# Block products for half of batch 6 as well, a denser two-batch product, and a written order for the last halves

## The chip, the cores and the metric

The kernel runs on one core of a Trainium2 chip. The metric is the device time of the whole program in microseconds. A run has one profiled execution, taken by the hardware profiler; its span goes from the first instruction to the last.

## The reference

```python
# _layernorm, gelu, rsqrt: the usual ones
def layer0(x, ada_emb):                    # x (8, 1024, 512), ada_emb (8, 512)
    ae = _layernorm(ada_emb, ln_g, ln_b)
    h = gelu(ae @ w1 + b1)
    x_a, x_b = split(h @ w2 + b2, 2)       # each (8, 512, 8)
    layer = base_layer + einsum('bdr,bkr->bdk', x_a, x_b)
    return x + einsum('btc,bco->bto', x, layer)

def layer1(x, y):
    ys = y / sqrt(512)
    d = rsqrt(einsum('bi,io->bo', ys * ys, weight * weight) + 1e-8)
    return einsum('bsi,io->bso', x * ys[:, None, :], weight) * d[:, None, :]

x = x + layer0(x, cond_1024)
out = x + layer1(x, cond_1024)
```

Everything after the small conditioning part is linear in x, so the kernel forms one 512 x 512 matrix per batch, q[b], and multiplies x[b] (1024 x 512) by it.

## The kernel before

Float32 products are made of three matmuls: each operand is split into a rounded part (ScalarE, a cast to float32r) and the rest (VectorE, a subtraction), and high x high, high x rest and rest x high are added in PSUM.

*Start.* The first 80 us load the weights, compute the conditioning and make q[0] to q[3]. This stretch is not touched by the change.

*Main tiles.* `main(b, t)` (L811) computes 128 rows of output: 4 chunks of the inner dimension x 3 = 12 matmuls of 512 columns into a `po` bank, a ScalarE copy, and a store of 256 KB issued by ScalarE. There are 8 tiles per batch; the text counts them through, tile 8b + t, from 0 to 55 for batches 0 to 6. `load_x` (L663) brings half a batch of x (1 MB) through SP's queue into the pool `big`, which has nine buffers; `split_x` (L667) splits the columns of two tiles. The matrices q[b] and the split x (`xs`) live in `big` as well. `split_p` (L651) splits q[b] into `ph` and `pl`.

*Making the next matrices.* Between main tiles, lists of work (`at`, L945) make q[4] to q[7]. `Pair` (L547) makes two batches' matrices, 4 with 5 and 6 with 7, by seven block products instead of eight, in the order `(1, 2, 5, 6, 3, 7, 4)`. A product has two units of six matmuls of 512 columns. `early` makes a right operand on VectorE, `prepare` rounds and splits it. Two units share banks of the pool `acc` (four banks): product 5 takes the banks of product 2 once VectorE has added those into q. One unit stands behind each main tile. `rank_term` (L514) adds the rank-8 part: four small matmuls (`pr`) into four `acc` banks and four additions on VectorE. `load_rank` (L505) fetches its operands by eight transfers that POOL issues, and `load_d` two rows for `Pair`.

*The last batch.* `Seven` (L823) computes batch 7 by seven block products with the Winograd form of Strassen's scheme, on blocks of half the inner dimension and half the columns. `make_right` makes four sums of blocks of q[7] and splits all right operands. `make_left(g)` does the same for x. `part(g)` runs the products in the order 1, 5, 6, 2, 7, 3, 4, each 12 matmuls of 256 columns, and writes 512 rows of output as two tiles `o1` and `o2` of 512 KB. Products 1, 6, 7 and 4 add onto one bank (`sw`), 5 and 3 onto another (`sz`), 2 has its own (`sv`). Between them the bank is read: a copy on ScalarE (L915, L917, L919, L928) or an addition on VectorE (L921, L923, L925). The block that follows on the same bank waits for that read. In the last part product 4 is copied and stored in two pieces (L912).

*Order.* TensorE's matmuls stand in text order. In the first 80 us VectorE and ScalarE do too (`InOrder.on`); from L805 on a scheduler orders them, with its own estimate of times. A wrapper `ve`, `se`, `sy` pins an instruction only while `InOrder.on` is set; `nc.vector` and `nc.scalar` are never pinned. Pools that the end needs (`late`) open when the pools of the making are closed (`late_pools`, L937).

Of the kernel before, what the change touches and what calls it, by code (L numbers as in the profile page):

```python
# [7 lines left out]
F32 = mybir.dt.float32  # L8
F32R = mybir.dt.float32r
# [5 lines left out]
P = 128  # L15
NB = 8
NT = 1024
D = 512
# [12 lines left out]
def cond_resid_kernel(ctx: ExitStack, tc: tile.TileContext, small, cond, condrows, consts,  # L31
# [791 lines left out]
    class Seven:  # L823
# [5 lines left out]

        ORDER = (1, 5, 6, 2, 7, 3, 4)

        def __init__(self, b):
            self.b, self.left = b, {}

        def make_right(self):
            b, late = self.b, pools["late"]
            t = late.tile([P, 4, 2, HD], F32R, tag="tl", name=f"tl_{b}", bufs=1)  # L840
            h = late.tile([P, 4, 2, HD], F32R, tag="th", name=f"th_{b}", bufs=1)
            raws = late.tile([P, 4, 2, HD], F32, tag="sums", name=f"traw_{b}", bufs=2)
            t1, t2, t3, t4 = (raws[:, i] for i in range(4))
            b11, b12 = q[b][:, 0:2, 0:HD], q[b][:, 0:2, HD:D]
            b21, b22 = q[b][:, 2:4, 0:HD], q[b][:, 2:4, HD:D]
            p_tiles(b)
            for rows, cols in ((slice(0, 4), slice(0, HD)), (slice(2, 4), slice(HD, D))):
                nc.scalar.copy(ph[b][:, rows, cols], q[b][:, rows, cols])
                nc.vector.tensor_sub(pl[b][:, rows, cols], q[b][:, rows, cols],
                                     ph[b][:, rows, cols].bitcast(F32))  # L850
            for o, x, y in ((t1, b12, b11), (t2, b22, t1), (t3, b22, b12), (t4, b21, t2)):
                nc.vector.tensor_sub(o, x, y)
            for i in range(0, 4, 2):
                at = slice(i, i + 2)
                nc.scalar.copy(h[:, at], raws[:, at])
                nc.vector.tensor_sub(t[:, at], raws[:, at], h[:, at].bitcast(F32))
            self.right = {5: (h[:, 0], t[:, 0]), 6: (h[:, 1], t[:, 1]), 7: (h[:, 2], t[:, 2]),
                          4: (h[:, 3], t[:, 3])}
            for p, rows, cols in ((1, slice(0, 2), slice(0, HD)), (2, slice(2, 4), slice(0, HD)),
                                  (3, slice(2, 4), slice(HD, D))):  # L860
                self.right[p] = ph[b][:, rows, cols], pl[b][:, rows, cols]

        def make_left(self, g):
            b, late = self.b, pools["late"]
            at = slice(2 * P * g, 2 * P * (g + 1))
            top, low = raw[b, 0][:, :, at], raw[b, 1][:, :, at]
            a11, a12, a21, a22 = top[:, 0:2], top[:, 2:4], low[:, 0:2], low[:, 2:4]
            s = late.tile([P, 4, 2, 2 * P], F32R, tag="sl", name=f"sl_{b}_{g}", bufs=2)
            h = late.tile([P, 4, 2, 2 * P], F32R, tag="sh", name=f"sh_{b}_{g}", bufs=2)
            x = late.tile([P, 2, 2, 2 * P], F32R, tag="x22", name=f"x22_{b}_{g}", bufs=2)  # L870
            xa = big.tile([P, 2, KC, 2 * P], F32R, tag="big", name=f"xa_{b}_{g}")
            nc.scalar.copy(xa[:, 0], top)
            nc.vector.tensor_sub(xa[:, 1], top, xa[:, 0].bitcast(F32))
            raws = late.tile([P, 4, 2, 2 * P], F32, tag="sums", name=f"sraw_{b}_{g}", bufs=2)
            s1, s2, s3, s4 = (raws[:, i] for i in range(4))
            nc.vector.tensor_add(s1, a21, a22)
            nc.vector.tensor_sub(s2, s1, a11)
            for i, (o, u, v) in enumerate(((s3, a11, a21), (s4, a12, s2))):
                nc.vector.tensor_sub(o, u, v)
            for i in range(0, 4, 2):  # L880
                two = slice(i, i + 2)
                nc.scalar.copy(h[:, two], raws[:, two])
                nc.vector.tensor_sub(s[:, two], raws[:, two], h[:, two].bitcast(F32))
            nc.scalar.copy(x[:, 0], a22)
            nc.vector.tensor_sub(x[:, 1], a22, x[:, 0].bitcast(F32))
            self.left[g] = {5: (h[:, 0], s[:, 0]), 6: (h[:, 1], s[:, 1]), 7: (h[:, 2], s[:, 2]),
                            3: (h[:, 3], s[:, 3]), 4: (x[:, 0], x[:, 1]),
                            1: (xa[:, 0, 0:2], xa[:, 1, 0:2]), 2: (xa[:, 0, 2:4], xa[:, 1, 2:4])}

        def product(self, g, p, bank, m, first):  # L890
            (lh, ll), (rh, rl) = self.left[g][p], self.right[p]
            for kk in range(2):
                for i, (a, r) in enumerate(((lh, rh), (lh, rl), (ll, rh))):
                    mm(bank[:, m, :], a[:, kk, m * P:(m + 1) * P], r[:, kk, :],
                       start=(first and m == 0 and kk == 0 and i == 0),
                       stop=(kk == 1 and i == 2), skip_group_check=True)

        def part(self, g, last):
            b, bank = self.b, {}
            o1, o2 = (pools["late"].tile([P, 2, D], F32, tag="o2", name=f"o{i}_{b}_{g}", bufs=3)  # L900
                      for i in range(2))
            for p in self.ORDER:
                key = {5: "z", 3: "z", 2: "v"}.get(p, "w")
                first = p in (1, 5, 2)
                if first:
                    pool, tag = (acc, "acc") if key == "v" else (po, "po")
                    bank[key] = pool.tile([P, 2, HD], F32, tag=tag, name=f"s{key}_{b}_{g}")
                u = bank[key]
                for m in range(2):
                    self.product(g, p, u, m, first)  # L910
                    if p == 4 and last:
                        nc.scalar.copy(o2[:, m, 0:HD], u[:, m])  # L912
                        self.store(o2, g, 1, slice(m, m + 1))
                if p == 1:
                    nc.scalar.copy(o1[:, :, 0:HD], u)  # L915
                elif p == 5:
                    nc.scalar.copy(o2[:, :, HD:D], u)  # L917
                elif p == 6:
                    nc.scalar.copy(o1[:, :, HD:D], u)  # L919
                elif p == 2:  # L920
                    nc.vector.tensor_add(o1[:, :, 0:HD], u, o1[:, :, 0:HD])  # L921
                elif p == 7:
                    nc.vector.tensor_add(o2[:, :, HD:D], u, o2[:, :, HD:D])  # L923
                elif p == 3:
                    nc.vector.tensor_add(o1[:, :, HD:D], u, o1[:, :, HD:D])  # L925
                    self.store(o1, g, 0, slice(0, 2))
                elif not last:
                    nc.scalar.copy(o2[:, :, 0:HD], u)  # L928
                    self.store(o2, g, 1, slice(0, 2))

        def store(self, o, g, half, ms):
            at = half * HT + 2 * P * g
            nc.scalar.dma_start(
                out[self.b, at + P * ms.start:at + P * ms.stop, :].rearrange("(m p) d -> p m d", p=P),
                o[:, ms, :])

# [15 lines left out]
    place = lambda i: divmod(i, NTT)  # L952
    for b in range(1, 4):
        first = (b - 1) * NTT
        at(*place(max(0, 4 * b - 8)), load_rank, b)
        at(*place(4 * b - 2), rank_term, b)
        for j in range(2):
            at(*place(first + 3 + j), split_p, b, j)
    for b, first in ((4, 13), (6, 30)):

        at(*place(first - 9), load_d, b)
        at(*place(first - 6), new_pair, b)
        for n, p in enumerate(Pair.ORDER):
            at(*place(first - 5 + 2 * n), lambda b=b, p=p: pairs[b].early(p))
            at(*place(first - 2 + 2 * n), lambda b=b, p=p: pairs[b].prepare(p))
            for i in range(2):
                at(*place(first + 2 * n + i), lambda b=b: pairs[b].unit())
        at(*place(first + 2), load_rank, b)
        at(*place(first + 4), load_rank, b + 1)
        at(*place(first + 14), rank_term, b)  # L970
        at(*place(first + 15), rank_term, b + 1)
        at(*place(first + 15), split_p, b, 0)
        at(*place(first + 16), split_p, b, 1)
        if b == 4:
            at(*place(first + 19), split_p, b + 1, 0)
            at(*place(first + 21), split_p, b + 1, 1)
    seven = Seven(NB - 1)
    at(*place(46), late_pools)
    at(*place(47), seven.make_right)
    at(*place(49), load_x, NB - 1, 0)  # L980
    at(*place(50), load_x, NB - 1, 1)
    at(*place(52), seven.make_left, 0)
    at(*place(54), seven.make_left, 1)

    for b in range(NB - 1):
        for t in range(NTT):
            if t == 0 and b + 2 < NB:
                p_tiles(b + 1)
            main(b, t)
            i = b * NTT + t  # L990
            if t % 4 == 0 and i + 4 < (NB - 1) * NTT:
                load_x(*divmod(i // 4 + 1, NHALF))
            if t % 2 == 0 and i + 4 < (NB - 1) * NTT:
                split_x(*divmod(i // 2 + 2, NTT // 2))
            for f, args in after.get((b, t), ()):
                f(*args)
    for g in range(2):
        seven.part(g, g == 1)


# [67 lines left out]
```

## Time and profile before

| | |
|---|---|
| median of 3 runs | 302.77 us (302.65 to 303.15) |
| profiled execution | 302.81 us |
| its span | 301.0 us |
| TensorE matmul, busy | 294.3 us, 1429 matmuls |
| VectorE, busy | 194.0 us, 287 instructions |
| ScalarE, busy | 150.2 us, 218 instructions |
| GpSimd, busy | 34.8 us |
| data moved | 62.12 MB, mean 206 GB/s |
| main tiles end, block products start | 276.35 us |

How to read it: PE is TensorE, PEld its weight loads, DVE VectorE, ACT ScalarE, POOL GpSimd; ACTq is the queue on which ScalarE issues transfers. The helper lines L45 and L62 record every matmul and most of the elementwise work, so groups are told apart by tiles: `po` main tiles, `pp` the two-batch products, `pr` rank terms, `sw`, `sz`, `sv` the block products of the end. `o` is an output tile in SBUF. A row of the timeline is start, duration, engine, line, operation and tiles, and in brackets the idle time before it with what ended it. Matmuls are pipelined, so that one takes longer (0.28 us) than the step to the next (0.12 us). The span's last TensorE matmul starts at 297.10.

### The profile page before, as it was taken

What the parts mean: (1) busy time and instruction counts of PE and PEld (TensorE: products, weight loads), DVE (VectorE), ACT (ScalarE), POOL (GpSimd) and SP (SyncE); (2) the same over time, 40 slices, a digit from 0 to 9 for tenths busy, and PEclk for the clock granted to TensorE, in tenths of its full rate; (3) what the DMA queues carried; (4) which work ended last, traced back from release to release, by engine and by line L of the source; (5) the groups of instructions that cost most, each with busy time, mean ns of one, the idle gap of its engine ahead of it and who ended that gap; (6) DMA issues with size and microseconds to landing.
All of it is one profiled execution on the core that took longest, in us unless ns stands there. A gap on an engine that the chain in (4) does not pass through costs nothing.

```text
span 301.0 us, 3809 instructions
## 1 busy us (share of the span) xinstructions
PE 294.3 (98%) x1429; PEld 224.8 (75%) x1429; DVE 194.0 (64%) x287; ACT 150.2 (50%) x218; POOL 34.8 (12%) x74
## 2 busy tenths in 40 slices
PE   7999999999999999999999999999999999999994
PEld 2655465466878778888888877888888877888993
DVE  4779750979569889794157549994356238994201
ACT  4756132256566672572457535664465436855130
POOL 0011000057104505100000018000000000000000
PEclk9999999999999999999999999999999999999999
DMA  6999999696519888186124347725144364432033
GB/s 207 412 426 418 407 423 416 216 327 182 197 70 312 320 250 273 72 244 210 69 89 193 87 192 188 233 82 199 50 194 152 128 209 140 165 117 93 12 143 139
DMA packets 19027, 62.12 MB, mean 206 GB/s; under 512 B 2736, under 2 KB 2992, under 8 KB 14656
## 3 DMA queue, kind: packets, MB, share of 16 engines
q1 hardware_dynamic: 6064, 38.78, 34.6%
q10 hardware_dynamic: 9168, 16.78, 15.0%
q0 software_dynamic: 3776, 6.31, 7.7%
q8 instruction: 11, 0.18, 0.2%
q14 instruction: 8, 0.07, 0.1%
HBM read 44.02 MB, written 17.84 MB: 206 GB/s over the span
## 4 chain that ended last, share of the span: by engine, by line
PE 86%; DMA 5%; DVE 5%; ACT 2%; issue 1%; SPq 0%; ACTq 0%
PE po L45 51%; PE pp L45 13%; PE pq L45 7%; PE sw L45 4%; DMA w<-in_w 4%; PE px L45 3%; PE pg L45 2%; PE sz L45 2%; DVE n L62 2%; DMA b_raw<-in_baseT 2%; PE pr L45 1%; PE sv L45 1%; PE pt_t L45 1%; ACT work L62 1%; DVE scr L62 0%
## 5 line engine op out<-in xcount | busy, mean ns | idle before, releaser
L45 PE MATMUL po<-ph,xs 128*128 128x512 f32 x448 | 144.9, 391 | 0.0
L45 PEld LDWEIGHTS po<-ph,xs 128*128 128x128 f32 x448 | 84.1, 188 | 19.3 <-issue 1.7
L45 PE MATMUL po<-pl,xs 128*128 128x512 f32 x224 | 87.3, 390 | 0.0
L62 ACT COPY o<-po 128x512 f32<-128x512 f32 x56 | 32.8, 586 | 60.8 <-PE po L45 60.8
L45 PEld LDWEIGHTS po<-pl,xs 128*128 128x128 f32 x224 | 42.1, 188 | 8.6
L62 DVE TENSOR_TENSOR xs<-x,xs 128x1024 fp32r<-128x1024 f32 x28 | 34.0, 1220 | 10.5 <-ACT xs L62 10.5
L62 DVE TENSOR_TENSOR nl_p<-n,nh_p 128x1024 fp32r<-128x1024 f32 x14 | 17.1, 1222 | 23.1 <-ACT nh_p L62 23.0
L62 ACT CAST xs<-x 128x1024 fp32r<-128x1024 f32 x28 | 29.1, 1052 | 1.2 <-DMA x<-in_x 1.0
L62 DVE TENSOR_TENSOR q<-pr,q 128x512 f32<-128x512 f32 x32 | 20.1, 684 | 13.6 <-PE pr L45 13.6
L511 POOL DMA_DIRECT2D fa<-kept_a x28 | 13.7, 506 | 77.9 <-PE pr L45 77.2
L45 PE MATMUL pq<-nh,bh 128*128 128x512 f32 x48 | 19.8, 412 | 0.0
L45 PE MATMUL pq<-nl,bh 128*128 128x512 f32 x48 | 19.1, 398 | 0.1
L62 ACT COPY q<-pp 128x512 f32<-128x512 f32 x20 | 11.7, 587 | 14.9 <-PE pp L45 14.1
L45 PE MATMUL pq<-nh,bl 128*128 128x512 f32 x48 | 18.9, 394 | 0.0
L62 DVE SCALAR_TENSOR_TENSOR n<-w_sb,ysT,d 128x512 f32<-128x512 f32 x24 | 17.7, 746 | 1.5 <-DMA d<-d_out 1.5
L62 DVE TENSOR_TENSOR pl<-q,ph 128x1024 fp32r<-128x1024 f32 x14 | 16.9, 1220 | 0.1
L62 ACT CAST nh_p<-n 128x1024 fp32r<-128x1024 f32 x14 | 14.7, 1052 | 3.5 <-DVE n L62 1.9
L62 ACT CAST ph<-q 128x1024 fp32r<-128x1024 f32 x14 | 14.6, 1053 | 3.4 <-DVE q L62 3.1
L45 PE MATMUL px<-w,hT 128*32 128x512 f32 x128 | 16.0, 601 | 0.1
L45 PEld LDWEIGHTS pq<-nh,bh 128*128 128x128 f32 x48 | 9.0, 188 | 8.4 <-issue 5.0
L511 POOL DMA_DIRECT2D ft<-kept_t x28 | 13.8, 512 | 4.9 <-DMA kept_t<-st_t 4.9
L62 ACT CAST nh<-n 128x512 fp32r<-128x512 f32 (+1 forms) x10 | 6.9, 707 | 11.5 <-DVE n L62 11.5
(193 smaller groups left out, 407.1 us busy)
## 6 DMA issues: line engine op xcount, KB each, us to landing
w<-in_w SPq DMA_DIRECT2D x16, 1024.0 KB, 10.7
x<-in_x SPq DMA_DIRECT2D x16, 1024.0 KB, 5.3
out<-o ACTq DMA_DIRECT2D x58, 256.0 KB, 2.1
ft<-kept_t POOLq DMA_DIRECT2D x28, 64.0 KB, 3.4
fa<-kept_a POOLq DMA_DIRECT2D x28, 64.0 KB, 3.2
d<-d_out POOLq DMA_DIRECT2D x6, 256.0 KB, 3.9
out<-o ACTq DMA_DIRECT2D x3, 512.0 KB, 2.9
w_sb<-in_weight SPq DMA_DIRECT2D x2, 512.0 KB, 5.3
```

What stands on the lines that cost most here:

```text
L45: tc.keep_in_program_order(nc.tensor.matmul(*args, **kw))
L62: return lambda *a, **kw: pin(f(*a, **kw)) if InOrder.on else f(*a, **kw)
L511: nc.gpsimd.dma_start(fold[name, b][32 * c:32 * c + 32, :], kept[name, g][32 * i:32 * i + 32, :])
```

## The change

The block products take over the second half of batch 6 (512 rows, main tiles 52 to 55) as well. `Seven` is made for batches 6 and 7, and a part now covers the rows of one half of x, `raw[b, g]`, where it had taken two columns of rows from both halves. `make_right` is divided into `make_sums` and the rest, which batch 6 doesn't need. `make_left` becomes a generator whose steps are put between the products of the part before it. There are three parts: batch 6 half 1, batch 7 half 0, batch 7 half 1. In these parts `InOrder.on` is set, and all elementwise work goes through `ve` and `se`. In the last part the bank `sw` becomes two banks, one for each 128 rows. The scratch pools change their number of buffers.

The product of batches 6 and 7 starts at tile 28 where it started at 30, and has three units per two tiles where it had two. That of 4 and 5 starts at tile 11 where it started at 13. The rank terms of batches 2 to 7, the splits of q[2] to q[6] and the opening of `late` move with them.

```diff
-        def make_right(self):
+        def make_sums(self):
...
-            t = late.tile([P, 4, 2, HD], F32R, tag="tl", name=f"tl_{b}", bufs=1)
-            h = late.tile([P, 4, 2, HD], F32R, tag="th", name=f"th_{b}", bufs=1)
-            raws = late.tile([P, 4, 2, HD], F32, tag="sums", name=f"traw_{b}", bufs=2)
+            t = late.tile([P, 4, 2, HD], F32R, tag="tl", name=f"tl_{b}", bufs=2)
+            h = late.tile([P, 4, 2, HD], F32R, tag="th", name=f"th_{b}", bufs=2)
+            raws = late.tile([P, 4, 2, HD], F32, tag="sums", name=f"traw_{b}", bufs=1)
...
         def make_left(self, g):
...
-            at = slice(2 * P * g, 2 * P * (g + 1))
-            top, low = raw[b, 0][:, :, at], raw[b, 1][:, :, at]
+            top, low = (raw[b, g][:, :, 2 * P * i:2 * P * (i + 1)] for i in range(2))
...
+            def rest(two):
+                ve.tensor_sub(s[:, two], raws[:, two], h[:, two].bitcast(F32))
+
+            se.copy(xa[:, 0], top)
+            se.copy(x[:, 0], a22)
+            ve.tensor_add(s1, a21, a22)
+            ve.tensor_sub(s2, s1, a11)
+            yield
+            se.copy(h[:, 0:2], raws[:, 0:2])
+            ve.tensor_sub(s3, a11, a21)
+            ve.tensor_sub(s4, a12, s2)
+            yield
+            se.copy(h[:, 2:4], raws[:, 2:4])
+            ve.tensor_sub(xa[:, 1], top, xa[:, 0].bitcast(F32))
+            yield
+            rest(slice(0, 2))
+            yield
+            ve.tensor_sub(x[:, 1], a22, x[:, 0].bitcast(F32))
+            yield
+            rest(slice(2, 4))
+            yield
...
+        def part(self, g, steps=(), last=False):
...
             for p in self.ORDER:
...
-                    pool, tag = (acc, "acc") if key == "v" else (po, "po")
-                    bank[key] = pool.tile([P, 2, HD], F32, tag=tag, name=f"s{key}_{b}_{g}")
...
+                    pool, tag = (po, "po") if key == "z" else (acc, "acc")
+                    bank[key] = [pool.tile([P, 2, HD], F32, tag=tag, name=f"s{key}{i}_{b}_{g}")
+                                 for i in range(2 if key == "w" and last else 1)]
+                self.product(g, p, bank[key], first)
...
+                for m, u in enumerate(bank[key]):
+                    u, to = (u, slice(0, 2)) if len(bank[key]) == 1 else (u[:, 0:1], slice(m, m + 1))
+                    if p in (2, 3, 7):
+                        ve.tensor_add(o[:, to, cols], u, o[:, to, cols])
+                    else:
+                        se.copy(o[:, to, cols], u)
+                    if p in (3, 4):
+                        self.store(o, g, int(p == 4), to)
+                next(steps, None)
...
-        at(*place(max(0, 4 * b - 8)), load_rank, b)
-        at(*place(4 * b - 2), rank_term, b)
+        at(*place(max(0, 3 * b - 7)), load_rank, b)
+        at(*place(3 * b - 1), rank_term, b)
...
-    for b, first in ((4, 13), (6, 30)):
+    for b, spots in ((4, [11 + n for n in range(14)]), (6, [28 + 2 * n // 3 for n in range(14)])):
...
+            spot = spots[2 * n]
+            at(*place(spot - 5), lambda b=b, p=p: pairs[b].early(p))
+            at(*place(spot - 2), lambda b=b, p=p: pairs[b].prepare(p))
+        for spot in spots:
+            at(*place(spot), lambda b=b: pairs[b].unit())
...
+        at(*place(end), rank_term, b)
+        at(*place(end + 1), rank_term, b + 1)
+    for b, spot in ((4, 26), (5, 33), (6, 41)):
+        for j in range(2):
+            at(*place(spot + j), split_p, b, j)
...
+    at(*place(40), late_pools)
+    at(*place(42), sevens[0].make_sums)
+    at(*place(43), sevens[0].make_right, True)
+    at(*place(44), load_x, NB - 2, 1)
+    at(*place(45), sevens[1].make_sums)
+    at(*place(47), all_left, 0, 1)
+    at(*place(48), sevens[1].make_right, False)
+    at(*place(48), load_x, NB - 1, 0)
...
+    load_x(NB - 1, 1)
+    InOrder.on = True
+    sevens[0].part(1, sevens[1].make_left(0))
+    sevens[1].part(0, sevens[1].make_left(1))
+    sevens[1].part(1, last=True)
```

## The prediction

> **What bounds the kernel now.** I read the page first (busy shares, slices, chain), then TensorE's matmul starts in order of time, then the busy time by stage around the last two batches, then the last 6 us on every engine and the DMA engines. The profiled execution took 302.81 us; its span is 301.0, so 1.8 us lie around the span. The median of the runs shown is 302.77, so sums made against the profile need a shift of only -0.04.
>
> ```profile
> PE 294.3 (98%) x1429; PEld 224.8 (75%) x1429; DVE 194.0 (64%) x287; ACT 150.2 (50%) x218; POOL 34.8 (12%) x74
> ...
> PE   7999999999999999999999999999999999999994
> ...
> PE 86%; DMA 5%; DVE 5%; ACT 2%; issue 1%; SPq 0%; ACTq 0%
> ```
>
> A busy TensorE is not yet a full one, so I looked at the matmul starts. From 80 us to 295.7 us they follow each other at a constant pitch per shape; the only longer steps are some 0.2 us around each group of four rank matmuls (pr). So in that stretch the time is the number and the shape of the matmuls, and VectorE and ScalarE cost something only where they make TensorE wait. Nothing in the first 88 us changes order.
>
> ```profile
> 180.00:230.00 50.00, 50.00 (x222) 40.80 (x221) 36.52 (x45) 28.22 (x37) 6.96 (x15) 1.00 0.46 151
> ...
> 265.47:276.35 10.88, 10.88 (x50) 9.01 (x48) 9.07 (x11) 5.72 (x8) 0.00 (x0) 1.00 0.27 99
> 276.35:286.43 10.08, 10.08 (x86) 10.08 (x85) 2.08 (x3) 2.35 (x4) 0.00 (x0) 1.00 0.07 28
> ```
>
> These are stretches of the span, with busy time of PE, PEld, DVE, ACT and POOL, then clock, DMA share and GB/s. The second is the last four tiles of batch 6, the third the first half of batch 7 by seven block products: the same amount of output, 10.88 us against 10.08. The clock is 1.00 in both. VectorE has much room in the third row.
>
> The last 6 us are another matter:
>
> ```profile
> 295.66 0.28 PE L45 MATMUL sw<-th,x 128*128 128x256 f32 x1
> 296.40 0.39 PE L45 MATMUL sw<-th,x 128*128 128x256 f32 x1 [0.46 <-ACT o L912]
> 297.10 0.28 PE L45 MATMUL sw<-th,x 128*128 128x256 f32 x1
> ```
>
> ```profile
> 295.98 0.37 ACT L912 COPY o<-sw 128x256 f32<-128x256 f32 x1 [4.45 <-DVE o L925]
> 295.99 0.90 ACTq L933 DMA_DIRECT2D out<-o  x2
> 297.42 0.37 ACT L912 COPY o<-sw 128x256 f32<-128x256 f32 x1 [1.07 <-PE sw L45]
> 297.82 0.35 ACTq L933 DMA_DIRECT2D out<-o  x1
> ```
>
> ```profile
> 296.00:297.00 1.00, 0.60 (x5) 0.60 (x6) 0.00 (x0) 0.35 (x1) 0.00 (x0) 1.00 0.11 41
> 297.00:298.00 1.00, 0.38 (x4) 0.18 (x2) 0.00 (x0) 0.37 (x1) 0.00 (x0) 1.00 1.03 389
> 298.00:299.00 1.00, 0.00 (x0) 0.00 (x0) 0.00 (x0) 0.00 (x0) 0.00 (x0) 1.00 1.01 375
> 299.00:300.00 1.00, 0.00 (x0) 0.00 (x0) 0.00 (x0) 0.00 (x0) 0.00 (x0) 1.00 0.65 244
> ```
>
> TensorE stands still between 295.78 and 296.40, because ScalarE reads the first half of the bank that the next matmuls write. The chain of waits runs through this stall. But the DMA rows say that the stall does not set the end: the stores of 512, 256 and 256 KB are 1 MB, and all 16 DMA engines are full from 296.9 to 299.65. That burst starts 0.9 us after the 512 KB store was issued at 295.99, and that store waits for VectorE's last addition (295.26 to 295.95). The last 256 KB, issued at 297.82, would begin to move at about 298.7 by the same 0.9 us. At 0.67 us for each 256 KB the two stores before it hold the engines from 296.9 to 298.9.
>
> **The change part by part.**
>
> *Four tiles of batch 6 become seven block products.* Removed: 4 x 12 = 48 matmuls of 512 columns, 10.88 us by the second row above, 227 ns each. Added: 7 x 12 = 84 of 256 columns, 10.08 us by the third row, 120 ns each. All of it lies on TensorE, which sets the time: -0.80 us. Rule against row: the trace has the pitch at 227 and 120 ns. The Trainium skill ("TensorE: Matmul & The Clock Gate", Back-to-back issue gap) gives an isolated pitch of columns / 2.4 GHz plus 2.5 ns, so 215.8 and 109.2 ns. By that the change would be worth 48 x 0.2158 - 84 x 0.1092 = 10.36 - 9.17 = 1.19 us. Each matmul here costs about 11 ns more than the rule, and the change adds 36 of them net; the row decides, 0.80.
>
> *Evictions and stores of those tiles.* Four ScalarE copies of 0.59 and four 256 KB stores go. Four copies, three VectorE additions of 0.69 and two 512 KB stores come, as in batch 7 today. They lie beside the products: 0.
>
> *Sums and splits for batch 6 (make_sums, make_left).* Batch 6's right sums are 4 x 0.69 + 2 x 1.22 = 5.2 us of VectorE and 2.1 of ScalarE. Its left half costs as much as one left half of batch 7, 4 x 0.69 + 3 x 1.22 + 0.69 = 7.1 us of VectorE and 3.8 of ScalarE. Two splits of x (1.22 each) go. In the built order the tile before the seam (tile 51, of 52) ends 13 tiles after the rank term of batch 7: 13 x 2.72 = 35.4 us. VectorE must do 2.5 (rank additions), ten instructions at a pitch of 1.13, thirteen at 0.60 and the right split of batch 7 (1.7) in it: 23.3 us. It also waits once for the stores of old tiles to land, because the late pools open there (about 2 us). I count left operands ready some 8 us before TensorE asks. Price 0, and without that cover TensorE would wait for the whole lateness.
>
> *Loads.* Halves of x now serve the seven products one by one, and the two for batch 7 are issued on SP in the same order as now. The buffer of each is free by tile 43 or earlier, a load lands in 5.3 us by the page, and its first reader is more than 15 us later: 0.
>
> *The two-batch product of 6 and 7 at three units per two tiles, and batches 1 to 5 earlier.* TensorE does the same 14 units (1.37 us each by six pitches of 228 ns); only the neighbours change. The cover shrinks: 9 tiles and 14 units are 43.7 us where 14 tiles and 14 units were 57.3. VectorE's load for it is 8 x 0.75 + 8 x 0.28 + 11 x 1.22 + 6 x 0.69 = 25.8 us, plus 5.5 for splits of x and 2.4 for the split of batch 5: 34 of 44 us. The tightest point is the first unit of product 5. Its bank is freed by the addition of product 2, the last of 20 VectorE instructions after the rank term of batch 4, at the pitches of the trace (four rank additions in 2.48 us, two splits in 2.35): 4 x 0.66 + 4 x 0.20 + 7 x 1.13 + 5 x 0.60 = 14.4, on top of that term's own additions (2.5): 16.9 us. TensorE has five tiles, four units and one rank term there, 13.6 + 5.5 + 0.6 = 19.7. Slack 2.8 us, price 0. The moved rank loads on POOL still wait for the same rank matmuls and are issued over ten us ahead of use: 0. Batches 4 and 5 start two tiles earlier, first unit near 115 us; their first split is ready by about 107: 0.
>
> *Text order in the last three halves.* Here ScalarE has to do four casts for the next half (1.05, 0.62, 1.05, 1.05) between its copies, in the order written. Rows for a copy, a cast of 1024 and one of 512:
>
> ```profile
> 254.97 0.58 ACT L62 COPY o<-po 128x512 f32<-128x512 f32 x1
> 255.45 1.05 ACT L848 CAST ph<-q 128x1024 fp32r<-128x1024 f32 x1
> 256.40 0.62 ACT L848 CAST ph<-q 128x512 fp32r<-128x512 f32 x1
> ...
> 277.98 0.59 ACT L915 COPY o<-sw 128x512 f32<-128x512 f32 x1 [0.85 <-PE sw L45]
> ...
> 280.86 0.59 ACT L919 COPY o<-sw 128x512 f32<-128x512 f32 x1 [0.85 <-PE sw L45]
> ```
>
> The pitches are 0.48 and 0.95, and about 0.52 for the short cast. A half starts at 0, and its first copy at 1.63 (277.98 - 276.35). Then: cast at 2.11, short cast 3.06, copy of product 5 at 3.58, cast 4.06, copy of product 6 at 5.01, done 5.60. Today that copy is at 4.51 and done at 5.10. Behind it waits product 7, which adds onto the same bank from 4 x 1.44 = 5.76. It fits by some 0.1 us. VectorE's chain: addition of product 2 at 6.03, the split at 6.63, addition of product 7 at 7.76 to 8.45, needed at 8.64; it fits by 0.2. This wait is not in the trace of before; bounds from both sides: 0 (none), and 0.5 us per half in the first two halves (the casts and the waits between them a tenth longer each), so 1.0. No gain is possible, as TensorE has no gaps there. I take 0 to 0.1, nearest to the rows.
>
> *Two banks for the last half's products.* They take away the 0.62 us stall. The Trainium skill ("PSUM — Partial Sum Buffer", PSUM bank collisions raise a hardware error) has PSUM guarded by bank and reading done from a different bank while matmuls run, which is what the edit does: by that, and by the chain, -0.62. By the DMA rows, 0: the 512 KB store still waits for the same addition, at the same distance from the end of product 3, and 1 MB still takes 2.75 us. I take 0 and keep -0.6 as the other end.
>
> Sum: -0.80 + 0 to 0.1 + 0 = -0.7 to -0.8 against 302.81; with the shift, 302.0 us.
>
> **The rivals.**
>
> *The end follows TensorE (0.09).* If the last 256 KB set the end, the 0.62 us comes on top: 301.4. For it: the chain runs through that stall. Against it: full DMA engines before the last store could begin.
>
> *The gain is mostly eaten by small waits (0.22).* ScalarE's order makes product 7 wait 0.2 to 0.4 us in each of two halves, or one unit of the dense two-batch product waits a little. For it: 0.1 us of margin. 302.2 to 302.7.
>
> *Slower (0.10): text order starves TensorE.* Place: product 7 behind the copy of product 6, in two halves. Price: twice the lateness beyond 0.12 us. A cast that comes 0.82 us late in each half costs 1.4 and gives 303.4; from there on it is slower by over 0.2%. For it: a pinned queue stops behind whatever is late, and the copy of product 5 in the second half also waits for a 512 KB store to land (2.9 us by the page, ready about 1 us before). Against it: the inputs of all the casts are long there.
>
> *The edit does not take effect.* It does: the built program has 36 more matmuls, and the block products stand where the four tiles stood.
>
> **How the numbers follow.** The likeliest case (0.59) gives 302.0, its own range 301.8 to 302.2. With the end following TensorE below it and the eaten gain above it, 301.3 to 302.7 leaves out the slower case and a little more. About 0.2% (0.6 us) is what a measurement of this kernel can tell from no change, so faster means below 302.17: nearly all of the likeliest case, all of the first rival, little of the second: 0.67. The rest of those: 0.23. Slower: 0.10.
>
> **What would show it.** Right: TensorE's starts without a gap until the last half; three halves of 10.08 us; the busy matmul time after the seam starting at about 265.5; the stall at the last product gone while the DMA engines are still full for 2.7 us after the last addition, and the end 0.8 us earlier. Wrong: gaps at product 7 put down to ScalarE; a gap before a unit of the product of 6 and 7 put down to VectorE; a half longer than 10.1 us; or a final burst that starts earlier after product 3 than 1.6 us.

## The result, and the profile after

| | before | after |
|---|---|---|
| median | 302.83 us (302.52 to 303.55, 22 runs) | 302.31 us (301.96 to 302.66, 22 runs) |
| ratio to before | | 0.9978, 95% interval 0.9972 to 0.9985 |
| span of the profiled execution | 301.0 us | 300.6 us |
| main tiles end, block products start | 276.35 | 265.65 |
| last half starts | 286.42 | 285.80 |

The change makes the kernel faster by 0.22%, or 0.67 us (0.45 to 0.85 by the interval); the two medians alone differ by 0.52 us. The 22 times of before include the three of the first table, and their median lies 0.06 above that of those three.

The busy shares, TensorE's slices and the chain of waits by engine, from the page of after:

```profile
PE 293.9 (98%) x1465; PEld 226.1 (75%) x1465; DVE 206.0 (69%) x303; ACT 152.8 (51%) x224; POOL 34.8 (12%) x74
...
PE   8999999999999999999999999999999999999993
...
PE 87%; DVE 5%; DMA 4%; ACT 2%; issue 0%; ACTq 0%
```

There are 36 matmuls more and 0.4 us less of TensorE. VectorE has 12 us more work, and the chain's share of it is still 5%, so that work is hidden. Where the time went is seen in the stretches (busy time of PE, PEld, DVE, ACT and POOL, then clock, DMA share, GB/s), with the borders at the starts of the three halves (the third row runs to the end of the last matmul, and so is longer than the pitches add up to):

```profile
265.65:275.72 10.07, 10.07 (x85) 10.07 (x84) 5.34 (x7) 5.50 (x8) 0.00 (x0) 1.00 0.08 28
275.72:285.80 10.08, 10.08 (x86) 10.08 (x85) 8.48 (x12) 5.50 (x8) 0.00 (x0) 1.00 0.28 106
285.80:296.04 10.24, 10.24 (x86) 10.04 (x84) 2.88 (x5) 2.85 (x7) 0.00 (x0) 1.00 0.27 102
```

Half of batch 6 takes 10.07 us now, where its four tiles took 10.88. In the two halves that prepare the next one ScalarE has 5.50 us of work where the first half had 2.35 before, and TensorE is busy without a break. From 80 us to the last matmul no step between matmuls is longer than the pitch of its shape, save the 0.2 us around rank terms that were there before.

The last instructions of ScalarE and its queue, and the DMA engines after them:

```profile
295.41 0.38 ACTq L62 DMA_DIRECT2D out<-o  x1
295.83 0.37 ACT L62 COPY o<-sw 128x256 f32<-128x256 f32 x1 [5.14 <-DVE o L62]
296.23 0.35 ACTq L62 DMA_DIRECT2D out<-o  x1
296.63 0.37 ACT L62 COPY o<-sw 128x256 f32<-128x256 f32 x1 [0.42 <-ACT o L62]
297.03 0.35 ACTq L62 DMA_DIRECT2D out<-o  x1
```

```profile
296.00:297.00 1.00, 0.04 (x1) 0.00 (x0) 0.00 (x0) 0.57 (x2) 0.00 (x0) 1.00 0.69 260
297.00:298.00 1.00, 0.00 (x0) 0.00 (x0) 0.00 (x0) 0.00 (x0) 0.00 (x0) 1.00 1.02 381
298.00:299.00 1.00, 0.00 (x0) 0.00 (x0) 0.00 (x0) 0.00 (x0) 0.00 (x0) 0.97 1.03 387
```

The last store is issued 11.23 us into the last half, where it was 11.40. But the 512 KB store is issued at 9.61, where it was 9.56; the DMA engines start 0.9 us after that and are full until 13.40, where it was 13.35. The shorter TensorE stretch at the end is not seen in the end.

Laid end to end, from the first main tile to the last half: 286.42 - 80.56 = 205.86 us before, 285.80 - 80.73 = 205.07 after, so -0.79. From the start of the last half to the end of the span: 14.62 before, 14.79 after, so +0.17. Together -0.62, and the ratio says -0.67. The first main tile itself starts anywhere from 80.3 to 81.2 us in the profiled executions of this study, whatever the kernel, so the -0.4 of the two spans is partly that.

### The profile page after: what moved, and what is told of

Same layout as the page of the kernel before. It is cut to its first block, busy times and chain, and to the rows that moved or that the text cites. A ratio compares the mean times of both kernels' runs of the same rounds, so it can differ in the third digit from the quotient of the medians.

```text
span 300.6 us, 3913 instructions
## 1 busy us (share of the span) xinstructions
PE 293.9 (98%) x1465; PEld 226.1 (75%) x1465; DVE 206.0 (69%) x303; ACT 152.8 (51%) x224; POOL 34.8 (12%) x74
## 4 chain that ended last, share of the span: by engine, by line
PE 87%; DVE 5%; DMA 4%; ACT 2%; issue 0%; ACTq 0%
PE po L45 48%; PE pp L45 13%; PE pq L45 7%; PE sw L45 5%; DMA w<-in_w 4%; PE px L45 3%; PE sz L45 3%; PE warm L45 2%; PE pg L45 2%; DVE n L62 2%; PE sv L45 1%; PE pr L45 1%; PE pt_t L45 1%; ACT work L62 1%; DVE scr L62 0%
## 5 line engine op out<-in xcount | busy, mean ns | idle before, releaser
L45 PE MATMUL po<-ph,xs 128*128 128x512 f32 x416 | 134.3, 392 | 0.0
L45 PEld LDWEIGHTS po<-ph,xs 128*128 128x128 f32 x416 | 78.1, 188 | 18.0 <-issue 1.7
L45 PE MATMUL po<-pl,xs 128*128 128x512 f32 x208 | 81.1, 390 | 0.0
L62 ACT COPY o<-po 128x512 f32<-128x512 f32 x52 | 30.5, 586 | 58.0 <-PE po L45 58.0
L45 PEld LDWEIGHTS po<-pl,xs 128*128 128x128 f32 x208 | 39.1, 188 | 8.0
L62 DVE TENSOR_TENSOR xs<-x,xs 128x1024 fp32r<-128x1024 f32 x26 | 31.5, 1221 | 10.5 <-ACT xs L62 10.4
L62 ACT CAST xs<-x 128x1024 fp32r<-128x1024 f32 x26 | 27.0, 1051 | 2.6 <-DMA x<-in_x 1.3
L62 DVE TENSOR_TENSOR pl<-q,ph 128x1024 fp32r<-128x1024 f32 (+1 forms) x16 | 18.8, 1189 | 6.9 <-ACT ph L62 6.8
L62 ACT CAST ph<-q 128x1024 fp32r<-128x1024 f32 (+1 forms) x16 | 16.2, 1027 | 2.1 <-DVE q L62 2.0
L62 ACT COPY o<-sw 128x512 f32<-128x512 f32 (+1 forms) x12 | 5.7, 480 | 15.7 <-PE sw L45 10.0
```

Of the source, the lines that this page charges most:

```text
L45: tc.keep_in_program_order(nc.tensor.matmul(*args, **kw))
L62: return lambda *a, **kw: pin(f(*a, **kw)) if InOrder.on else f(*a, **kw)
```

## The experiments

All ratios are to runs of the kernel before on the same chip and in the same group. The groups' medians of before were 302.84 (the first four experiments), 302.96 (short cast twice, new places alone, old places, the first version with all of batch 6), 302.87 (text order taken away, the second version with all of batch 6) and 302.98 (the third).

### The changed kernel again

> The changed kernel itself, as the yardstick of this group. Both theories: about 0.6 us under the kernel before (302.2 to 302.4). If the 0.17 us by which TensorE's first main tile came later in the profile of the changed kernel (80.73 us against 80.56) was chance, it differs in this profile; if it belongs to the kernel, it is there again.

302.37 us, ratio 0.9983 (0.9975 to 0.9992). From the first main tile to the last half 205.04 us, from there to the end 14.78. The parts of the time repeat to 0.04 us; what varies is the start of the first tile.

### One bank in the last half

```diff
-                                 for i in range(2 if key == "w" and last else 1)]
-                self.product(g, p, bank[key], first)
+                                 for i in range(1)]
+                halves = [(0,), (1,)] if last and p == 4 else [(0, 1)]
+                self.product(g, p, bank[key], first, halves[0])
```

> The changed kernel, with one bank instead of two for the products 1, 6, 7 and 4 of the last half, and product 4 computed, copied and stored in two pieces as before. Theory (the burst of 1 MB sets the end): TensorE stands still for about 0.6 us inside product 4 again, the last 256 KB store is issued 0.7 us later, and the time is the same within 0.15 us, as the DMA engines are full with the 768 KB before it. Rival (the end follows TensorE): 0.6 us slower than the changed kernel.

302.44 us, ratio 0.9985 (0.9979 to 0.9992). TensorE's rows of this kernel at the last product:

```profile
295.31 0.28 PE L45 MATMUL sw<-th,x 128*128 128x256 f32 x1
296.48 0.39 PE L45 MATMUL sw<-th,x 128*128 128x256 f32 x1 [0.89 <-ACT o L62]
```

The step between these two is 1.17 us where the pitch is 0.12, so the stall is back with 1.05 us. It is longer than the 0.62 of before, because in text order the copy that frees the bank stands behind the issue of the 512 KB store. The end of the span comes 14.92 us after the start of the last half, 0.13 to 0.14 later than with two banks. So 1.05 us of TensorE's stall cost 0.13 us of time: the burst of stores covers the rest.

### Stores of the last half cut by columns, with two banks and with one

Each block of columns is stored as soon as it is done, so that less than 1 MB is left for the end.

```diff
-                    if p in (3, 4):
+                    if not last and p in (3, 4):
                         self.store(o, g, int(p == 4), to)
+                    if last and p in (2, 3, 4):
+                        self.store(o, g, int(p == 4), to, cols)
+                if last and p == 7:
+                    self.store(o, g, 1, slice(0, 2), cols)
```

> The changed kernel, with the stores of the last half cut by columns, each piece stored as soon as it is complete: after product 2 and after product 7 a quarter of the output (256 KB) each, after product 3 a quarter, after product 4 two eighths. The burst behind product 3 is 512 KB instead of 1 MB. Theory (the burst sets the end): TensorE the same, the end 0.9 us earlier (packets end at 12.5 us after the start of the last half instead of 13.4, then set by the last piece's issue at 11.2 plus 0.9 of latency plus 0.36); if rows of 1 KB move at half the rate of rows of 2 KB, 0. Rival (the last copy and the latency of its store set the end, whatever else is in flight): no change, as that store is issued at the same moment.

> The stores cut by columns as in the run split_store, with one bank as in the run one_bank. Theory: without the long burst the stall of TensorE in product 4 is no longer covered, so this is 0.6 to 0.7 us slower than split_store, where one_bank costs nothing against the changed kernel. Rival (the stall never matters, because the final waits cost the same): as fast as split_store. Rival (the stall always matters): the same difference of 0.6 in both pairs.

Two banks: 301.47 us, ratio 0.9951 (0.9939 to 0.9964). One bank: 302.00, ratio 0.9967 (0.9955 to 0.998). The stretches at the end, first with two banks, then with one (each has its own start of the last half, 285.91 and 285.36):

```profile
294.00:295.00 1.00, 1.00 (x10) 1.00 (x10) 0.25 (x1) 0.00 (x0) 0.00 (x0) 1.00 0.58 197
295.00:296.00 1.00, 1.00 (x10) 0.95 (x8) 0.45 (x1) 0.06 (x1) 0.00 (x0) 1.00 0.53 181
296.00:297.00 1.00, 0.15 (x2) 0.00 (x0) 0.00 (x0) 0.58 (x2) 0.00 (x0) 1.00 0.56 193
297.00:298.00 1.00, 0.00 (x0) 0.00 (x0) 0.00 (x0) 0.11 (x1) 0.00 (x0) 1.00 0.61 202
```

```profile
296.00:297.00 1.00, 0.75 (x6) 0.54 (x5) 0.00 (x0) 0.21 (x1) 0.00 (x0) 1.00 0.97 331
297.00:298.00 1.00, 0.00 (x0) 0.00 (x0) 0.00 (x0) 0.16 (x1) 0.00 (x0) 1.00 0.04 13
298.00:299.00 1.00, 0.00 (x0) 0.00 (x0) 0.00 (x0) 0.00 (x0) 0.00 (x0) 1.00 0.39 131
```

With cut stores the DMA engines are no longer full from the first store to the end: the share is near 0.6 in every row of the first fence, because the pieces come with breaks between them (the longest 0.8 us), and only the last piece fills the engines again (0.94 from 298.0 to 298.3). The packets end 12.60 us into the last half where they ended at 13.40 (-0.80), and the end of the span is at 13.87 where it was at 14.79: 0.92 us earlier. The other 0.12 lies behind the last landing, which is taken up below. With one bank the share falls to 0.04 before the last 128 KB come: the engines wait for the late store. The same stall of 1.05 us that cost 0.13 under the burst costs 14.46 - 13.87 = 0.59 here (0.53 by the medians). So the two banks are worth little where the burst of stores sets the end, and half a microsecond and more where it does not.

### The short cast twice

```diff
             se.copy(xa[:, 0], top)
             se.copy(x[:, 0], a22)
+            se.copy(x[:, 0], a22)
```

> The changed kernel, with the short cast of x (the cast to x22) issued twice in the first step of each left half, so that ScalarE has one more cast of about 0.52 us pitch in front of the copies of products 5 and 6 in each of the first two seven-product halves of the end. The output is unchanged. Theory (ScalarE's text order has a margin of 0.14 us at product 7 and none to give beyond it): the copy of product 6 is done 0.52 later, product 7 waits 0.52 - 0.14 = 0.38 us in each of two halves, the halves take about 10.45 instead of 10.07, and the time is 0.76 above the changed kernel: about 303.1, slightly slower than the kernel before. Rival (the order is not tight, because ScalarE catches up before product 7): halves of 10.08 and the time of the changed kernel, 302.35.

303.59 us, ratio 1.0021 (1.0012 to 1.0029): slower than before. The halves take 10.71 and 10.72. ScalarE in the first of them (start, duration), then TensorE at product 7:

```profile
268.49 1.27 ACT L62 CAST x<-x 128x512 fp32r<-128x512 f32 x2
269.67 0.58 ACT L62 COPY o<-sz 128x512 f32<-128x512 f32 x1
270.15 1.05 ACT L62 CAST sh<-sraw 128x1024 fp32r<-128x1024 f32 x1
271.09 0.58 ACT L62 COPY o<-sw 128x512 f32<-128x512 f32 x1
```

```profile
271.06 0.28 PE L45 MATMUL sv<-ph,xa 128*128 128x256 f32 x1
271.73 0.38 PE L45 MATMUL sw<-th,sh 128*128 128x256 f32 x1 [0.39 <-ACT o L62]
```

The two casts take 1.18 us from the start of the first to the start of the copy behind them, where one took 0.52, so the second costs 0.66, not 0.52. The copy of product 6 starts 271.09 - 265.43 = 5.66 us into the half instead of 5.01. Product 7 starts 0.55 late, and the first matmul after the wait takes 0.10 more than the pitch; 0.64 per half, two halves 1.28. The mechanism is the expected one, and the rival falls; the expected size was 0.76 because I took the step from a cast to a copy for the step from a cast to a cast, and no price for the restart. One short cast more at this place in each of two halves turns the gain into a loss.

### The new places alone

The kernel before, with only these lines of the change, and the places of the splits that go with them:

```diff
-        at(*place(4 * b - 2), rank_term, b)
+        at(*place(3 * b - 1), rank_term, b)
...
-    for b, first in ((4, 13), (6, 30)):
+    for b, spots in ((4, [11 + n for n in range(14)]), (6, [28 + 2 * n // 3 for n in range(14)])):
```

> The kernel before, with only the new places of the two-batch product of 6 and 7 (three units per two tiles), of the rank terms and of the splits of the operator; batch 6 keeps its sixteen tiles and the last half its one bank. Theory (TensorE does the same matmuls in another order and VectorE has 2.8 us of slack): no steps between matmuls beyond those of the kernel before, and its time, 302.8 to 302.9. Rival A (the new places themselves gave some of the gain): 302.2 to 302.6. Rival B (they cost something that the seven products made good): 303.1 or more.

303.00 us, ratio 1.0002 (0.9994 to 1.0011). From the first main tile to the last half 287.12 - 81.20 = 205.92 us (205.86 before), and no new step between matmuls. The denser product costs nothing and gives nothing by itself.

### Seven products with the old places

```diff
-    at(*place(40), late_pools)
-    at(*place(42), sevens[0].make_sums)
+    at(*place(46), late_pools)
+    at(*place(47), sevens[0].make_sums)
```

and the product of 6 and 7, the rank terms and the splits where they are in the kernel before.

> The changed kernel with seven products for half of batch 6, but the two-batch product of 6 and 7 in the places that it has in the kernel before (one unit per tile, to the end of tile 43), and so the late pools after tile 46 instead of 40. Theory (the denser two-batch product is what buys VectorE its time): VectorE has some 22 us of work and a wait for stores between the opening of the pools and the last left operand, and six tiles, 16 us, to do it in; TensorE waits 2 to 9 us, most likely 5, at the first of the seven-product halves, so about 307. Rival (the new places are not needed): 302.4.

310.49 us (5 runs), ratio 1.0252 (1.0238 to 1.0266). The theory holds in direction, and the loss of about 8 us lies in its range of 2 to 9, above its middle. The place is another than I had said. The first half starts on time, at 265.72, and its own left operands suffice until product 7. ScalarE and TensorE there:

```profile
270.60 1.99 ACT L62 CAST th<-traw 128x1024 fp32r<-128x1024 f32 x2
275.53 1.04 ACT L62 CAST sh<-sraw 128x1024 fp32r<-128x1024 f32 x1 [2.94 <-DVE sraw L62]
276.48 0.58 ACT L62 COPY o<-sw 128x512 f32<-128x512 f32 x1
```

```profile
271.61 0.28 PE L45 MATMUL sv<-ph,xa 128*128 128x256 f32 x1
277.11 0.58 PE L45 MATMUL sw<-th,sh 128*128 128x256 f32 x1 [5.22 <-ACT o L62]
277.49 0.42 PE L45 MATMUL sw<-tl,sh 128*128 128x256 f32 x1
```

VectorE is late with the sums of the *next* half. In text order the cast of those sums stands ahead of the copy of product 6, behind two casts of batch 7's right sums that are late as well (1.99 us), and product 7 waits for that copy: 5.4 us. This is the starvation that the prediction had as its rival with the loss. With the new places VectorE has room here: the same sums are ready 5.8 us before their cast in the first half (263.88 and 269.71) and 2.0 us before it in the second, as these rows of the changed kernel show.

```profile
277.12 0.69 DVE L62 TENSOR_TENSOR sraw<-sraw,x 128x512 f32<-128x512 f32 x1
279.79 1.06 ACT L62 CAST sh<-sraw 128x1024 fp32r<-128x1024 f32 x1
```

With the old places that room is gone, and VectorE's lateness goes on into TensorE. What follows is a second price:

```profile
277.00:278.00 1.00, 0.89 (x4) 0.89 (x5) 1.00 (x2) 1.00 (x2) 0.00 (x0) 0.50 0.00 0
278.00:279.00 1.00, 1.00 (x7) 1.00 (x7) 1.00 (x2) 0.00 (x1) 0.00 (x0) 0.50 0.00 0
279.00:280.00 1.00, 1.00 (x6) 1.00 (x6) 0.56 (x1) 0.00 (x0) 0.00 (x0) 0.50 0.00 0
```

The granted clock (the column after POOL) is 0.50 for 3 us after the stall, and the steps are 0.21 us instead of 0.12. Some 13 matmuls at 0.09 more are about 1.2 us of the 7.06 that this half is longer.

### Text order taken away

```diff
-    InOrder.on = True
     sevens[0].part(1, sevens[1].make_left(0))
```

> The changed kernel, with the instructions of the three last halves left to the scheduler instead of text order. In the built program ScalarE then copies product 6 before the cast (earlier by one cast), VectorE does the sums and splits of the next half ahead of its additions, and in the last half the 512 KB store stands behind the copy of the first piece of product 4. Theory (the halves have room in either order; the end is set by when the last 1 MB begins to move): halves of 10.07 to 10.1 as before, but the 512 KB store is issued about 10.4 instead of 9.6 us into the last half, so the burst and the end come 0.8 later: about 303.1. Rival A (order does not matter): 302.35. Rival B (VectorE's order makes TensorE wait for an addition in the halves): a half longer than 10.3, and 303.5 or more.

302.39 us, ratio 0.9984 (0.9978 to 0.9991): the time of the changed kernel. The halves take 10.07 and 10.08; rival A holds and my theory falls. It rested on a misreading of the tail. The copy of the first piece of product 4 ran at 10.03 in the changed kernel, and I took that as the time when it could run. In the trace without text order:

```profile
295.05 0.37 ACT L62 COPY o<-sw 128x256 f32<-128x256 f32 x1 [4.67 <-DVE o L62]
295.13 0.91 ACTq L62 DMA_DIRECT2D out<-o  x2
```

It runs at 295.05 - 285.49 = 9.56, and the 512 KB store behind it is issued at 9.64, only 0.03 later than in text order. The 10.03 was the issue of the store ahead of it. So the written order neither gave nor cost time in the changed kernel; the copy of product 6, which it puts at 5.01, runs at 4.51 without it (269.85 - 265.34).

### All of batch 6 by seven products

48 tiles, then four halves, on top of the stores cut by columns; `late` opens after tile 38.

```diff
-    TILES = (NB - 1) * NTT - HALF
+    TILES = (NB - 2) * NTT
...
+    p_tiles(NB - 1)
+    sevens[1].make_right(False)
+    sevens[0].part(0, sevens[0].make_left(1))
     sevens[0].part(1, sevens[1].make_left(0))
```

> The version that cuts the stores of the last half by columns, with seven products for both halves of batch 6 (48 tiles, then four halves), late pools after tile 38. Theory (each half of four tiles turned into seven products is worth 48 x 0.227 - 84 x 0.120 = 0.80 us as long as the operands are ready): left operands are ready about 252 to 253, the first product starts near 254.8, halves of 10.07, and 301.5 - 0.8 = 300.7. Rival (VectorE is late without the four tiles of cover): TensorE waits 1 to 4 us at the first half, so 301.5 to 304.

302.91 us, ratio 0.9998 (0.999 to 1.0006): the gain expected did not come, and at first sight the rival holds. The first half took 11.70 us and the third 10.39. ScalarE in the first half (which starts at 254.62):

```profile
255.82 1.57 ACT L62 CAST ph<-q 128x1024 fp32r<-128x1024 f32 x2 [0.41 <-ACT o L62]
257.29 0.58 ACT L62 COPY o<-sw 128x512 f32<-128x512 f32 x1
```

Batch 7's right split (`ph<-q`) could not be made earlier, as its tiles were those of batch 5's operator, in use to the last tile; it stood in text order ahead of the copy of product 1, which should have run at 256.2. The next kernel gives it tiles of its own, from `big`:

```diff
+        if b == NB - 1:
+            ph[b], pl[b] = big_tile(f"ph_{b}", F32R), big_tile(f"pl_{b}", F32R)
+            return
...
+    at(*place(45), p_tiles, NB - 1)
+    at(*place(45), sevens[1].make_right, False)
...
-    p_tiles(NB - 1)
-    sevens[1].make_right(False)
```

> The version with seven products for all of batch 6 again, but batch 7's right split (two casts on ScalarE, two subtractions on VectorE) has tiles of its own instead of those that batch 5 uses to the last, and is done five microseconds before the first half instead of inside it. Theory (the first half of the version before waited 1.6 us because these casts, 1.57 us, stand in ScalarE's text order ahead of the first copies, not because the left operands were late; they were ready some 8 us before): first half 10.1 instead of 11.7, and 302.9 - 1.6 = 301.3, with the 0.3 us that the third half waits for a store to land still in it. Rival (VectorE or the operands were late): first half 11.5 or more, 302.8.

301.08 us (6 runs), ratio 0.9945 (0.9931 to 0.996). The first half takes 10.07 us: the rival falls. The third takes 10.85. ScalarE in it:

```profile
279.09 0.59 ACT L62 COPY o<-sz 128x512 f32<-128x512 f32 x1 [0.67 <-DMA out<-o]
279.57 1.05 ACT L62 CAST sh<-sraw 128x1024 fp32r<-128x1024 f32 x1
```

The copy of product 5 waits for the 512 KB store of the half before to land, whose tile it writes. The transfers in that stretch (queue, packets, MB, share of the engines; then the issues, with the median us from issue to landing), of this kernel:

```profile
q8 instruction: 1, 0.02, 2.0%
issues: line engine op xcount, KB each, median us to landing
out<-o ACTq DMA_DIRECT2D x1, 512.0 KB, 4.7
```

In the changed kernel the 512 KB stores at this place take 2.9 us. Here one transfer of 16 KB of instructions (q8) began together with the stores and took 1.7 us; after the burst the rest came at 15 to 31 GB/s, about one engine's share, until 15.0 us after the half's start instead of 13.4. That this transfer held the store up is read from the traces; no run moved it. Two other kernels point the same way: with all of batch 6, in the first version and in the next one, such a transfer stands at this place too, and the store lands 4.2 us after its issue; one half earlier, where none stands, it lands after 2.9 in both. One more tile of that kind, and one less for batch 5:

```diff
-            o1, o2 = (pools["late"].tile([P, 2, D], F32, tag="o2", name=f"o{i}_{b}_{g}", bufs=3)
+            o1, o2 = (pools["late"].tile([P, 2, D], F32, tag="o2", name=f"o{i}_{b}_{g}", bufs=4)
...
-        pools["o"] = ctx.enter_context(tc.tile_pool(name="opool2", bufs=4))
+        pools["o"] = ctx.enter_context(tc.tile_pool(name="opool2", bufs=3))
```

> The version with seven products for all of batch 6 and batch 7's right split in tiles of its own, with four instead of three output tiles for the block products (and three instead of four for the tiles of batch 5 at the end, so that the memory suffices). Theory (in the version before, the copy of product 5 in the third half waits 0.67 us for a 512 KB store of the half before to land, because its tile is that store's; with a fourth tile the store has half a half more): all three halves 10.07 to 10.10, and 301.1 - 0.77 = 300.3. Rival (three tiles for batch 5 make ScalarE wait for stores in its last tiles): a step between matmuls before the first half, 300.5 to 301.5.

300.94 us (5 runs), ratio 0.9933 (0.992 to 0.9947). The 16 KB transfer of instructions is at the same place, and nothing waits for it any more; all halves follow without a gap:

```profile
254.80:264.87 10.07, 10.07 (x85) 10.07 (x84) 6.42 (x9) 5.50 (x8) 0.00 (x0) 1.00 0.10 36
264.87:274.94 10.07, 10.07 (x86) 10.07 (x85) 8.48 (x12) 5.51 (x8) 0.00 (x0) 1.00 0.28 104
274.94:285.02 10.08, 10.08 (x86) 10.08 (x85) 8.49 (x12) 5.51 (x8) 0.00 (x0) 1.00 0.29 106
285.02:295.26 10.24, 10.24 (x86) 10.04 (x84) 2.88 (x5) 2.83 (x7) 0.00 (x0) 1.00 0.43 155
```

From the first main tile to the last half it takes 285.02 - 80.75 = 204.27 us, and 205.10 (285.91 - 80.81) with half of batch 6: -0.83, by the trace a second time the 0.80 of four tiles. From there to the end it is 14.00 instead of 13.87. The medians agree less well: 300.3 was expected, and the ratio is 0.18% below that of the cut stores alone, 0.5 us, with intervals that overlap. It is the fastest version here, 0.67% below the kernel before.

## Why the prediction was right, point by point

- *Four tiles become seven products, -0.80.* Right. The stretches give 10.88 and 10.07 us, -0.79 from first tile to last half, and -0.83 when a second four tiles are replaced. The -1.19 from the Trainium skill ("TensorE: Matmul & The Clock Gate", Back-to-back issue gap) does not show: the pitch stays at 0.12 us for 256 columns in all three halves.
- *Sums and splits, 0.* Right, with two wrong sizes under it. The left operands of the first half were ready at 260.82, 4.8 us before the half began, where I had counted "some 8"; my own terms, 35.4 - 23.3 - 2, even give 10. Most of the difference is the wait for old stores when `late` opens: "about 2 us" was 5.45, as VectorE's row shows. The price stayed at 0 because the cover was long enough for that error too.

```profile
242.58 1.30 DVE L62 TENSOR_TENSOR traw<-q 128x512 f32<-128x512 f32 x2 [5.45 <-DMA out<-o]
```

  How little cover there was is shown by the old places: six tiles less of it, and TensorE stands still.
- *The denser two-batch product, 0.* Right. By itself it moves nothing (1.0002). At its tightest point VectorE's addition of product 2 ends at 190.59 and the unit of product 5 starts at 193.44, so 2.85 us of slack (2.8 counted).
- *Text order, 0 to 0.1 (bound 1.0).* Right: 0. The rows in the first half, which starts at 265.65:

```profile
269.23 0.59 ACT L62 COPY o<-sz 128x512 f32<-128x512 f32 x1
269.71 1.06 ACT L62 CAST sh<-sraw 128x1024 fp32r<-128x1024 f32 x1
270.66 0.60 ACT L62 COPY o<-sw 128x512 f32<-128x512 f32 x1
```

```profile
271.28 0.29 PE L45 MATMUL sv<-ph,xa 128*128 128x256 f32 x1
271.40 0.29 PE L45 MATMUL sw<-th,sh 128*128 128x256 f32 x1
```

  The copy of product 6 starts at 5.01 and is done at 271.26, 0.14 us before product 7: the counted place to 0.01 us. VectorE's addition of product 7 ends at 274.03 and product 4 starts at 274.28. The short cast twice bears this out: 0.66 us more on ScalarE made product 7 start 0.55 late, so 0.11 us were free.
- *Two banks, 0 (other end -0.62).* Right. The burst sets the end; by the traces one bank costs 0.13 us under it (0.07 by the medians) and 0.5 to 0.6 without it. The rival in which the end follows TensorE was wrong for this kernel, and right for the one with cut stores.
- *The sum.* -0.7 to -0.8 was forecast and -0.62 to -0.67 came. The median of 302.31 lies above the likeliest case (301.8 to 302.2) and, as a number, in the range of the rival in which small waits eat the gain (302.2 to 302.7). The traces speak against that rival: no wait at product 7, and none at a unit of the two-batch product. The term that was left at zero is the tail: "the end 0.8 us earlier" missed +0.17 us. Of it, 0.05 is that the 512 KB store is issued later after its addition, 0.01 the burst itself, and 0.11 lies behind the last landing: from there to the end of the span it takes 1.04 us in the changed kernel and 0.93 before. In the trace SyncE goes through two more waits of 0.06 us in that stretch. That these make the 0.11 is read from the trace alone; no run took them away. The kernels with cut stores have 0.92 there (half of batch 6) and 1.04 (all of it).

## What to carry to other kernels

Where TensorE has no gaps, as here, a change of shape is worth its matmuls times the pitch of the trace; it was worth that a second time when it was repeated. What has to be checked for it is the cover of VectorE before the seam, and the order on ScalarE. There a cast for the next half stands ahead of a copy for this one: by the rows of the changed kernel 0.14 us of lateness on ScalarE, or 2.0 us on VectorE's sums in the second half, are free, and what went beyond in the two experiments stalled TensorE. At the end of a kernel ask which of TensorE and the stores is last. Here cutting the stores gave 0.9 us by the medians of one group (302.37 to 301.47); the second bank gave 0.07 without that and 0.5 with it.

## What the runs showed of the hardware that was not expected

- After 5.2 us of idleness TensorE's granted clock was 0.50 for about 3 us; after stalls of 0.55 and 1.05 us the steps were back at 0.12 us from the second matmul on. The Trainium skill ("TensorE: Matmul & The Clock Gate", Part 1: The HAM clock gate) has the clock fall after an idle window of about 3.4 us; both rows agree with that, and no run here has a stall between 1.05 and 5.2 us that would show the limit itself.
- The first matmul behind a wait takes 0.22 us to the next instead of 0.12, in the stalls of 0.55 us (short cast twice), 0.62 us (before) and 1.05 us (one bank).
- A transfer of 16 KB of instructions beside two 512 KB stores went with a landing 4.7 us after the issue instead of 2.9 (the version with all of batch 6, tiles of its own for the right split), and 4.2 us in the two other versions with all of batch 6. The margin of about 1 us that the changed kernel has there (issue at 275.26, landing 2.9 later, copy of product 5 at 279.31) did not survive that.
- SyncE's waits behind the last landing cost 0.06 us each in the trace, and how many there are differs: two more in the changed kernel than before.
